# Graph network layer: scores and sums in four TensorE column groups of 16 nodes over three tiles, with norms by two chunks

## The chip, the cores and the metric

The kernel runs on one core of one Trainium2 chip. The metric is the device time of one execution in microseconds: the median of 3 runs for the kernel before. Profiles show one execution each; its engines are TensorE (PE, with PEld for its weight loads), VectorE (DVE), ScalarE (ACT), GpSimd (POOL) and SyncE (SP), whose queue issues most DMAs.

## What is computed

Two graph convolutions with attention (TransformerConv, two heads of 64) over 6250 nodes and 106250 edges, a batch norm with ReLU between them, then a residual and a layer norm. All is float32; the edges come sorted by their destination `dst`.

```python
def _transformer_conv(h, edge_attr, src, dst, Wq, bq, Wk, bk, Wv, bv, We, Ws, bs):
    q, k, v = ...                      # h @ W + b, (n, 2, 64) each
    e = (edge_attr @ We).reshape(-1, H, C)
    alpha = jnp.einsum('ehc,ehc->eh', q[dst], k[src] + e) / jnp.sqrt(C)
    ex = jnp.exp(alpha - segment_max(alpha, dst)[dst])
    a = ex / segment_sum(ex, dst)[dst]
    out = segment_sum((v[src] + e) * a[:, :, None], dst)
    return out.reshape(n, H * C) + h @ Ws + bs

edge_attr = concat([cos((last_update[src] - t)[:, None] * time_w + time_b), msg])   # 32 + 64 columns
h = relu(batch_norm(_transformer_conv(x, edge_attr, ..., conv 1)))
out = layernorm(x + _transformer_conv(h, edge_attr, ..., conv 2))
```

## The kernel before, in words

The 106250 edges are cut into NC = 104 chunks of CE = 1024, a chunk into T = 8 tiles of 128 edges. A chunk is answerable for NN = 64 nodes, that is 128 rows of (node, head). As edges are sorted, the nodes of a chunk lie close together, and a plan at the start (`tile_gnn_resnorm`, L1303) works out from `dst` the first node of each group of nodes (`nbs`). It also checks that each node's edges lie in the tiles that its group looks at. Where that doesn't hold, the program takes `general`, another way altogether; `ordered` (L660) is the way that the profile shows.

A chunk's 64 nodes stand in two groups of GN = 32, 64 rows each. Group 0 looks at the last tile of the chunk behind and tiles 0 to 3, group 1 at tiles 3 to 7 (`window`, L687): five tiles for each. The first and the last chunk have windows of their own.

`conv(c, ...)` (L710) runs twice, c = 0 and c = 1. Its loop is a pipeline written out by hand (L1025 on); in iteration k stand, in this order on each engine:

- `fetch` (L740) of chunk k + 4 (c = 0) or k + 3 (c = 1): SyncE reads the groups' first nodes into registers (`value_load`, L747) and issues the loads of edge attributes (L751), one of query tables for each group (`ftab`, L767), and in the second convolution the time encoding (`fz`, L770), the turned attributes (`fxT` from `et_d`, L772) and two of residual rows (`fr`, L775).
- `gather` (L777) of the same chunk: eight indirect DMAs, issued by GpSimd, one for each tile, that bring the rows of the source nodes (L782). They are spread over the iteration, each tied to a step of TensorE by a dependence, so that they keep its pace.
- `score` (L867) of chunk k, in two halves (u = 0 and 1) into one PSUM tile of two banks: each group's 64 rows against five tiles, first the gathered rows (`ft`, 128 deep), then the attributes (`et`, 112 deep). A group writes its own 64 columns of TensorE.
- `turn_weights` (L908) of chunk k - 1: five 128x128 transposes of the weights in two PSUM tiles, copied by ScalarE.
- `divide` and `finish_turn` (L934, L948) of chunk k - 2: sums over their denominators, then two transposes.
- `lowest` and `weigh` (L896, L903) of chunk k: a minimum over the scores on VectorE and an exponential on ScalarE, 640 columns each.
- `turn_in` (L843) of chunk k + 1, in two halves: transposes of the gathered rows, and in the first convolution of the attributes too, copied by ScalarE (L856, L862); the turned attributes are stored to `et_d` (L864) for the second convolution.
- `finish` (L957) of chunk k - 2: products with Wv and We. In the first convolution the node's skip values, third column of the table, are added, and two stores of 32 nodes each into `hT` are put on a list (`outgoing`). In the second the residual is added, the row centred and its square summed. The norms of ten chunks (LG = 10, `STARTS`) are finished together: one square root on ScalarE (L1005), a reciprocal, and then `store` (L1010) scales a chunk's rows and puts two stores of 32 rows on the list.
- `gather_sums` (L920) of chunk k - 1: weights times gathered rows and attributes, 225 columns, for two groups and five tiles.

`send()` (L729) takes the next store off the list and puts it into SyncE's queue. It is called at four fixed places of an iteration. Stores into `out` and into `hT` wait for the one before to have landed, since neighbouring groups may overlap.

`tables` (L621) makes the query tables block by block between these steps, `tab_d` in DRAM, three columns for each head of a node in the first convolution (against the gathered rows, against the attributes, and skip) and two in the second. After the last iteration of the second convolution comes a tail written out by hand (L1117 to L1151).

Of the kernel before, what the change touches and what calls it, by code (L numbers as in the profile page):

```python
# [7 lines left out]
F32 = mybir.dt.float32  # L8
# [39 lines left out]
GN = NN // 2  # L48
NC = 104
NG = 2 * NC  # L50
# [10 lines left out]
LG = 10  # L61
STARTS = (*range(0, 91, LG), 96, 100, 102, 103)
# [558 lines left out]
def tables(nc, pl, c, fT, b0, work, bank):  # L621

    o = work.tile([P, GE, H, 3 - c], F32, name="fo", tag="fo", bufs=1)
    for i, (a, b) in enumerate(pl.mats[c]):
        pg = bank()
        pl.step = nc.tensor.matmul(pg, a, fT, start=True, stop=True)  # L626
        if i == 2 * H:
            nc.scalar.activation(o[:, :, :, 2], pg[:, :, None].to_broadcast([P, GE, H]), AF.Identity, bias=b)
# [6 lines left out]
        if i == len(pl.mats[c]) - 1:  # L635
            nc.scalar.dma_start(pl.tab_d[c][:, b0 * GE:(b0 + 1) * GE], o)
# [23 lines left out]
def ordered(ctx: ExitStack, tc: tile.TileContext, pl, x, dst, edge_attr_64, conv2, bn_g, bn_b, out):  # L660
# [23 lines left out]
    def bounds(j):  # L684
        return max(0, N - GN * (NG - j)), min(N - NN, GN * j)

    def window(k, g):  # L687
        if k == 0:
            return range(3 * g, 3 * g + GT + 1)
        if k == NC - 1:  # L690
            return range(4 * g - 4, 4 * g + GT - 1)
        return range(GT * g - 1, GT * g + GT)
# [4 lines left out]
    nc.vector.memset(qpi, HALF_PI)  # L697

# [11 lines left out]
    def conv(c, extra, first_blocks=None):  # L710
# [8 lines left out]
        p_s = cs.enter_context(tc.tile_pool(name=f"fp_s{c}", bufs=1, space=bass.MemoryType.PSUM))  # L719
# [14 lines left out]
        groups = [slice(g * NN, (g + 1) * NN) for g in range(2)]  # L734
        halves = [slice(g * GN, (g + 1) * GN) for g in range(2)]
# [4 lines left out]
        def fetch(k):  # L740
            s = ch[k] = Plan()
            s.behind = ch.get(k - 1)
            s.nb = []
            for j in (2 * k, 2 * k + 1):
                lo, hi = bounds(j)
                s.nb.append(lo if lo == hi else N - GN * (NG - j) if j >= NG - 2 else
# [18 lines left out]
            s.tab = load.tile([P, NN * H, 3 - c], F32, name="ftab")  # L765
            for g, r in enumerate(groups):
                nc.sync.dma_start(s.tab[:, r], pl.tab_d[c][:, bass.ds(s.nb[g], GN)].rearrange("p n h w -> p (n h) w"))  # L767
            if c:
# [5 lines left out]
                for r, at in zip(halves, s.nb):  # L774
                    nc.sync.dma_start(s.r[r], res_d[bass.ds(at, GN), :])  # L775
# [91 lines left out]
        def score(k, u):  # L867

            s = ch[k]
            if u == 0:  # L870
                s.bank = p_s.tile([P, CE], F32, name="fps")
                s.ps = s.bank[:, CE - len(window(k, 0)) * P:]
                s.runs = [[], []]
                for g, r in enumerate(groups):
                    tiles = window(k, g)
# [633 lines left out]
```

## Time and profile before

| | us |
|---|---|
| median of 3 runs | 2253.65 (2251.95 to 2262.63) |
| the profiled execution, whole | 2255.35 |
| its span, first to last instruction | 2253.5 |
| mean granted TensorE clock | 0.934 of full |

```
## 2 busy tenths in 40 slices
PE   4888889978888988988878888888788887887865
POOL 3777777777777777777277777777777777777750
DMA  7776666656676667766397666666666666666641
```

The page gives each engine's busy time, its share of the span and its instructions; here the span in 40 slices, each digit a tenth. Issuing and waiting don't count as busy. The dip in slices 20 and 21 is the passage from the first convolution to the second. A row of a group of instructions has its line, engine and operation, what it writes and reads, its count, its busy time, the mean of one in ns, and then the idle time of the engine ahead of it with what ended it.

### The profile page before, as it was taken

The numbers are of one execution on the slowest core, as the hardware profiler recorded it, in microseconds if no ns is written. First come the engines' busy times: TensorE is split into PE (matmuls) and PEld (weight loads), VectorE is DVE, ScalarE is ACT, GpSimd is POOL, SyncE is SP. The second block draws the span as 40 slices with busy tenths as digits, with TensorE's granted clock in tenths as the row PEclk, the third lists the DMA queues.
The fourth block names the chain that finished last, engine by engine and source line by source line (L and its number), as shares of the span: only waits on it lengthen the run. The fifth ranks groups of instructions, "written<-read, shape, count | busy, mean of one in ns | idle before, by whom it ended". The sixth has DMA issues, their size and how long they took to land.

```text
span 2253.5 us, 44949 instructions
## 1 busy us (share of the span) xinstructions
PE 1852.5 (82%) x13283; PEld 1254.6 (56%) x13283; DVE 1148.7 (51%) x3686; ACT 1099.8 (49%) x1947; POOL 1590.8 (71%) x1683
## 2 busy tenths in 40 slices
PE   4888889978888988988878888888788887887865
PEld 3565666656665666666545565555554555554433
DVE  4766666766666667777454333333333333333322
ACT  1767676755655555666533434343333333333323
POOL 3777777777777777777277777777777777777750
PEclk9999999989999999999889999999999999999987
DMA  7776666656676667766397666666666666666641
GB/s 220 199 196 182 167 182 193 188 148 176 191 191 185 161 188 196 190 174 176 84 259 186 176 174 167 173 169 181 171 176 164 174 176 182 163 167 149 160 120 45
DMA packets 476600, 389.76 MB, mean 173 GB/s; under 512 B 295438, under 2 KB 422306, under 8 KB 473018
## 3 DMA queue, kind: packets, MB, share of 16 engines
q1 hardware_dynamic: 404262, 235.05, 38.7%
q0 software_dynamic: 53184, 109.45, 20.5%
q10 hardware_dynamic: 18900, 42.28, 5.2%
q8 instruction: 109, 1.79, 0.4%
q14 instruction: 145, 1.19, 0.2%
HBM read 271.26 MB, written 111.89 MB: 170 GB/s over the span
## 4 chain that ended last, share of the span: by engine, by line
DMA 23%; PE 21%; issue 4%; SPq 3%; DVE 3%; POOL 1%; ACT 1%; ACTq 0%; DVEq 0%; POOLq 0%
DMA fxT<-et_d 14%; PE fps L890 7%; DMA ff<-hn_d,fsrcs 5%; PE fpa L930 4%; PE fppt L916 3%; PE fpx L852 3%; DMA out<-fout 2%; SPq L767 1%; POOL ff L782 1%; PE fpo L986 1%; PE fpo L952 1%; PE fpg L626 1%; SPq L770 1%; DMA ff<-h_d,fsrcs 1%; DMA ff<-xv_d,fsrcs 1%
## 5 line engine op out<-in xcount | busy, mean ns | idle before, releaser
L782 POOL DMA_INDIRECT ff<-xv_d,fsrcs x831 | 798.9, 961 | 283.4 <-issue 91.4
L782 POOL DMA_INDIRECT ff<-hn_d,fsrcs x783 | 742.1, 948 | 267.1 <-issue 91.8
L930 PE MATMUL fpa<-ff,fpt 128*64 128x225 f32 x4176 | 461.7, 364 | 1.7 <-ACT fpt L917 1.7
L890 PE MATMUL fps<-fft,ftab 128*64 128x512 f32 (+1 forms) x1668 | 361.3, 462 | 49.9 <-DMA ftab<-tab_d 42.0
L856 ACT COPY fft<-fpx 128x512 f32<-128x512 f32 x404 | 235.5, 583 | 287.6 <-PE fpx L852 287.1
L930 PEld LDWEIGHTS fpa<-ff,fpt 128*64 128x64 f32 x4176 | 335.2, 140 | 59.4 <-issue 3.5
L955 DVE COPY fat<-fpo 128x256 f32<-128x256 f32 x208 | 88.4, 425 | 532.7 <-PE fpo L953 520.6
L917 ACT COPY fpt<-fppt 128x384 f32<-128x384 f32 (+1 forms) x416 | 156.7, 428 | 395.0 <-PE fppt L916 390.0
L852 PE MATMUL fpx<-fident,ff 128*128 128x128 f32 x1664 | 273.3, 295 | 53.1 <-DMA ff<-hn_d,fsrcs 44.7
L852 PEld LDWEIGHTS fpx<-fident,ff 128*128 128x128 f32 x1664 | 215.2, 152 | 68.9 <-DMA ff<-hn_d,fsrcs 53.9
L890 PE MATMUL fps<-fxT,ftab 112*64 112x512 f32 (+1 forms) x834 | 168.0, 476 | 97.1 <-DMA fxT<-et_d 97.1
L916 PEld LDWEIGHTS fppt<-fident,fs 128*128 128x128 f32 x1044 | 116.1, 146 | 178.6 <-issue 154.7
L890 PEld LDWEIGHTS fps<-fft,ftab 128*64 128x64 f32 x1668 | 132.4, 156 | 139.3 <-issue 96.7
L906 ACT ACTIVATE fs<-fps,fm 128x640 f32<-128x640 f32 x208 | 165.8, 797 | 39.6 <-DVE fm L901 37.7
L952 PE MATMUL fpo<-fident,fa 128*128 128x128 f32 x208 | 68.9, 331 | 139.3 <-DVE fa L940 137.2
L899 DVE TENSOR_REDUCE flow<-fps 128x1 f32<-128x640 f32 x208 | 170.1, 818 | 13.3 <-PE fps L890 13.3
L916 PE MATMUL fppt<-fident,fs 128*128 128x128 f32 x1044 | 168.6, 295 | 8.1 <-DVE fb L600 4.7
L890 PEld LDWEIGHTS fps<-fxT,ftab 112*64 112x64 f32 x834 | 59.7, 149 | 176.1 <-DMA fxT<-et_d 160.2
L890 PE MATMUL fps<-fet,ftab 112*64 112x512 f32 (+1 forms) x834 | 153.2, 434 | 0.0
L861 PE MATMUL fpe<-fident,ff 128*112 128x128 f32 x832 | 143.2, 301 | 2.4 <-DVE ff L839 2.2
L834 ACT ACT_TABLE_LOAD x82 | 105.2, 1283 | 76.0 <-issue 74.0
L827 DVE SCALAR_TENSOR_TENSOR farg<-fturns,farg 128x256 f32<-128x256 f32 x312 | 132.9, 426 | 10.7
(202 smaller groups left out, 2367.7 us busy)
## 6 DMA issues: line engine op xcount, KB each, us to landing
ff<-in_edge_attr SPq DMA_DIRECT2D x206, 256.0 KB
et_d<-fet SPq DMA_DIRECT2D x104, 448.0 KB
fxT<-et_d SPq DMA_DIRECT2D x104, 448.0 KB
tab_d<-fo ACTq DMA_DIRECT2D x13, 1536.0 KB
ftab<-tab_d SPq DMA_DIRECT2D x208, 96.0 KB
enc_d<-fzs SPq DMA_DIRECT2D x104, 128.0 KB
tab_d<-fo ACTq DMA_DIRECT2D x13, 1024.0 KB
ftab<-tab_d SPq DMA_DIRECT2D x208, 64.0 KB
```

The source lines that it names most:

```text
L782: row = nc.gpsimd.indirect_dma_start(out=f[:, t, (1 if c else 0):1 + D], out_offset=None, in_=(h_d[:N, :] if k < RAW else hn_d) if c else ...
L827: nc.vector.scalar_tensor_tensor(arg, turn, -part, arg, op0=OP.mult, op1=OP.add)
L834: nc.scalar.activation(z[:, :len(of)], arg[:, :len(of)], AF.Sin, bias=qpi)
L852: last = nc.tensor.transpose(px[:, t * P:(t + 1) * P], s.f[:, u * 4 + t, 1:1 + D], ident)
L856: nc.scalar.copy(s.ft[:, u * GE:(u + 1) * GE], px)
L861: last = nc.tensor.transpose(pe[:EC, t * P:(t + 1) * P], s.f[:, u * 4 + t, 1 + D:], ident)
L890: step = nc.tensor.matmul(s.bank[r, to:to + n], s.tab[:kd, r, i], (of.et if i else of.ft)[:kd, at:at + n], start=i == 0, stop=i == 1)
L899: nc.vector.tensor_reduce(low, s.ps, AX.X, OP.min)
L906: nc.scalar.activation(s.s[:, :s.ps.shape[1]], s.ps, AF.Exp, bias=s.bias, scale=-1.0)
L916: last = nc.tensor.transpose(pp[:, at:at + P], s.s[:, t * P:(t + 1) * P], ident)
L917: nc.scalar.copy(s.pt[:, t0 * P:t1 * P], pp[:, :(t1 - t0) * P])
L930: steps.append(nc.tensor.matmul(s.pa[r], s.pt[:, t * P + g * NN:t * P + (g + 1) * NN], f[:, i % T, 1:1 + D + EW], start=t == 0, stop=t == ...
```

## The change

Four groups of 16 nodes take the place of two of 32: 32 rows and 32 columns of TensorE each (GH), over three tiles: group g looks at tiles 2g - 1, 2g and 2g + 1. So scores, minimum, exponential and weights are 384 columns wide, not 640; a chunk's scores are made at one place, into one of two PSUM tiles of one bank, in an order that takes the groups in turn. The first nodes of two neighbouring groups lie at most 16 apart and can lie closer; then two groups hold the same nodes. A 0/1 matrix made for each chunk on VectorE (`sel`, from `target`, made once by `targets`) joins the groups' rows: `finish_turn` multiplies with it where it transposed before, and what comes out are 64 neighbouring nodes from the chunk's first. So residual rows are one load, `hT` and `out` one store a chunk. The skip column leaves the tables for a tensor of its own. Norms are finished by two chunks, with a small exponential (`spare`) right behind the square root, and the places of `send` and of the gathers' ties move. The plan works with four groups.

```diff
-GN = NN // 2
+NQ = 4
+GN = NN // NQ
+GH = P // NQ
+QE = CE // NQ
 NC = 104
-NG = 2 * NC
+NG = NQ * NC
...
-LG = 10
-STARTS = (*range(0, 91, LG), 96, 100, 102, 103)
+LG = 2
+STARTS = (*range(0, NC - 2, LG), NC - 2, NC - 1)
...
-    o = work.tile([P, GE, H, 3 - c], F32, name="fo", tag="fo", bufs=1)
+    o = work.tile([P, GE, H, 2], F32, name="fo", tag="fo", bufs=1)
     for i, (a, b) in enumerate(pl.mats[c]):
         pg = bank()
         pl.step = nc.tensor.matmul(pg, a, fT, start=True, stop=True)
         if i == 2 * H:
-            nc.scalar.activation(o[:, :, :, 2], pg[:, :, None].to_broadcast([P, GE, H]), AF.Identity, bias=b)
+            skip = work.tile([P, GE], F32, name="fskip", tag="fskip", bufs=1)
+            nc.scalar.activation(skip, pg, AF.Identity, bias=b)
+            nc.scalar.dma_start(pl.skip_d[:, b0 * GE:(b0 + 1) * GE], skip)
...
-        return max(0, N - GN * (NG - j)), min(N - NN, GN * j)
+        return max(0, N - GN * (NG - j)), min(N - GN if j % NQ else N - NN, GN * j)
 
     def window(k, g):
-        if k == 0:
-            return range(3 * g, 3 * g + GT + 1)
         if k == NC - 1:
-            return range(4 * g - 4, 4 * g + GT - 1)
-        return range(GT * g - 1, GT * g + GT)
+            return range(2 * g - 3, 2 * g + 1)
+        return range(max(2 * g - 1, 0 if k == 0 else -1), 2 * g + 2 + (k == g == 0))
...
+            none = gt.tile([P, NC], F32, name="fnone")
+            nc.vector.tensor_scalar(none, pg[:, 1, :NC], float(H), own, op0=OP.mult, op1=OP.is_le)
+            nc.vector.tensor_scalar(target, pg[:, 0, :NC], float(H), own, op0=OP.mult, op1=OP.add)
+            nc.vector.scalar_tensor_tensor(target, none, float(P), target, op0=OP.mult, op1=OP.add)
...
-        p_s = cs.enter_context(tc.tile_pool(name=f"fp_s{c}", bufs=1, space=bass.MemoryType.PSUM))
+        p_s = cs.enter_context(tc.tile_pool(name=f"fp_s{c}", bufs=2, space=bass.MemoryType.PSUM))
...
+            if c:
+                send()
             s.nb = []
-            for j in (2 * k, 2 * k + 1):
+            for j in range(NQ * k, NQ * k + NQ):
...
-            s.tab = load.tile([P, NN * H, 3 - c], F32, name="ftab")
+            s.tab = load.tile([P, NN * H, 2], F32, name="ftab")
             for g, r in enumerate(groups):
                 nc.sync.dma_start(s.tab[:, r], pl.tab_d[c][:, bass.ds(s.nb[g], GN)].rearrange("p n h w -> p (n h) w"))
+            if c == 0:
+                s.skip = load.tile([P, NN], F32, name="fsk")
+                nc.sync.dma_start(s.skip, pl.skip_d[:, bass.ds(s.nb[0], NN)])
             if c:
                 s.z = load.tile([P, T, TD], F32, name="fz", bufs=AHEAD)
                 nc.sync.dma_start(s.z, enc_d[k].rearrange("p (t d) -> p t d", d=TD))
                 s.et = ets[k % len(ets)]
                 nc.sync.dma_start(s.et, et_d[k])
                 s.r = load.tile([NN, D], F32, name="fr", bufs=6)
-                for r, at in zip(halves, s.nb):
-                    nc.sync.dma_start(s.r[r], res_d[bass.ds(at, GN), :])
+                nc.sync.dma_start(s.r, res_d[bass.ds(s.nb[0], NN), :])
+                send()
...
+            n = len(window(k, 0)) * P
+            s.ps = p_s.tile([P, GE], F32, name="fps")[:, :n]
+            todo = []
+            for g, r in enumerate(groups):
+                tiles, at = window(k, g), 0
+                for own in (False, True):
+                    part = [t for t in tiles if (t >= 0) == own]
+                    for i in range(2 if part else 0):
+                        todo.append((at, g, r, s if own else s.behind, i, tiles.index(part[0]) * P, part[0] % T * P, len(part) * P))
+                        at += len(part) * P
+            steps = []
+            for _, _, r, of, i, to, at, n in sorted(todo, key=lambda one: one[:2]):
+                kd = EC if i else D
+                steps.append(nc.tensor.matmul(s.ps[r, to:to + n], s.tab[:kd, r, i], (of.et if i else of.ft)[:kd, at:at + n],
+                                              start=i == 0, stop=i == 1))
+            half, step = steps[NQ - 1], steps[-1]
...
+            n = len(window(k, 0))
+            pp = p_tr.tile([P, GE], F32, name="fppt", tag="tr")
+            for t in range(n):
+                last = nc.tensor.transpose(pp[:, t * P:(t + 1) * P], s.s[:, t * P:(t + 1) * P], ident)
+            nc.scalar.copy(s.pt[:, :n * P], pp[:, :n * P])
...
-                    steps.append(nc.tensor.matmul(s.pa[r], s.pt[:, t * P + g * NN:t * P + (g + 1) * NN],
+                    steps.append(nc.tensor.matmul(s.pa[r], s.pt[:, t * P + g * GH:t * P + (g + 1) * GH],
                                                   f[:, i % T, 1:1 + D + EW], start=t == 0, stop=t == n - 1))
-            return steps[2], steps[5], steps[-1]
+            return steps[3], steps[7], steps[-1]
...
+            s.sel = small.tile([P, P], F32, name="fsel", bufs=2)
+            nc.vector.tensor_scalar(s.sel, place_of, target[:, k:k + 1], None, op0=OP.is_equal)
...
-            nc.tensor.transpose(s.po[:, 0], s.a[:, :D], ident)
-            nc.tensor.transpose(s.po[:, 1], s.a[:, EW:], ident)
+            nc.tensor.matmul(s.po[:, 0], s.a[:, :D], s.sel, start=True, stop=True)
+            step = nc.tensor.matmul(s.po[:, 1], s.a[:, EW:], s.sel, start=True, stop=True)
...
-                    nc.vector.tensor_add(res[r], heads[r, :, h], s.tab[r, ::H, 2])
+                    nc.vector.tensor_add(res[r], heads[r, :, h], s.skip[r])
...
-                    for r, at in zip(halves, s.nb):
-                        outgoing.append((hT[:, bass.ds(at, GN)], res[:, r]))
+                    outgoing.append((hT[:, bass.ds(s.nb[0], NN)], res))
...
+                if k < NC - 2:
+                    spare = small.tile([1, 1], F32, name="fspare", bufs=2)
+                    nc.scalar.activation(spare, pl.ones[0:1, 0:1], AF.Exp)
...
-            for r, to in zip(halves, at):
-                outgoing.append((out[bass.ds(to, GN), :], o[r]))
+            outgoing.append((out[bass.ds(at, NN), :], o))
...
-                send()
+                if not c:
+                    send()
+                elif not coming:
+                    send(2)
...
-                step = score(k, 0)[1] if on(k) else None
+                half, scored = score(k) if on(k) else (None, None)
                 if k >= -1 and not filling:
-                    bring((1,), step)
+                    bring((1,), half)
...
-                half, step = score(k, 1) if on(k) else (None, None)
-                if k >= -1 and not filling:
-                    bring((3,), half if c else step or half)
-                    if c:
-                        bring((4,), step)
-                send()
-                if on(k - 2):
-                    finish_turn(k - 2)
                 if on(k):
                     lowest(k)
+                if not c:
+                    send()
+                if on(k - 2):
+                    step = finish_turn(k - 2)
+                if k >= -1 and not filling:
+                    bring((3,), step)
                 step = turn_in(k + 1, 0) if on(k + 1) else None
-                if k >= -1 and not c or filling:
+                if k >= -1:
                     bring(range(5) if filling else (4,), step)
...
-                for _ in range(min(len(done), 4 if k >= NC else 2 if k > NC - 12 else 1)):
+                for _ in range(min(len(done), 2 if k > NC - 6 else 1)):
                     store(*done.pop(0))
-                if c:
-                    send()
...
-                spare = small.tile([1, 1], F32, name="fspare", bufs=1)
-                nc.scalar.activation(spare, pl.ones[0:1, 0:1], AF.Exp)
                 turn_in(last, 1)
-                score(last, 0)
-                score(last, 1)
+                score(last)
```

Left out are the plan's checks for four groups in `tile_gnn_resnorm` (eight picked columns of `dst` in place of four, rows of 416 in place of 208), the rest of `targets` (the distances of the first nodes, spread over 128 rows by eight products of one row) and changes of names.

168 lines of the change are left out of this document (85 added, 83 removed).

## Prediction

> **What bounds the kernel now.** I read the page first, for its spread of work over engines, and it points the wrong way.
>
> ```profile
> span 2253.5 us, 44949 instructions
> PE 1852.5 (82%) x13283; PEld 1254.6 (56%) x13283; DVE 1148.7 (51%) x3686; ACT 1099.8 (49%) x1947; POOL 1590.8 (71%) x1683
> ```
>
> TensorE looks like the bound and GpSimd (POOL) like the runner-up. So the second view is the one line that GpSimd works at, the row gathers of L782, then the same line by stage (us, busy us and count), then GpSimd in order of time.
>
> ```profile
> L782 POOL DMA_INDIRECT ff<-xv_d,fsrcs x831: 940/944/1188, 32.8 to 1084.7; - x167
> L782 POOL DMA_INDIRECT ff<-hn_d,fsrcs x783: 938/944/1707, 1183.5 to 2191.5; - x196
> L782 POOL DMA_INDIRECT ff<-h_d,fsrcs x48: 940/944/1986, 1121.7 to 1182.3; - x48
> ```
> ```profile
> 33.00:1086.00 1053.00, 798.68 (x831) 0.94 0.67 181
> 1121.00:1250.00 129.00, 97.86 (x100) 0.90 0.82 218
> 1250.00:1460.00 210.00, 159.05 (x168) 0.93 0.65 170
> 1700.00:2140.00 440.00, 319.84 (x339) 0.96 0.64 167
> 2140.00:2193.00 53.00, 31.21 (x34) 0.87 0.47 118
> ```
> ```profile
> 1121.67 0.94 POOL L782 DMA_INDIRECT ff<-h_d,fsrcs  x1 [36.07 <-issue]
> 1122.92 0.94 POOL L782 DMA_INDIRECT ff<-h_d,fsrcs  x1 [0.30 <-issue]
> ...
> 2185.19 0.94 POOL L782 DMA_INDIRECT ff<-hn_d,fsrcs  x1 [2.54 <-PE fps L890]
> ```
>
> A gather is 0.94 us, and 0.30 us lie ahead of it even where nothing is waited for: from start to start 1.25 us. There are 831 + 783 + 48 = 1662, eight to a chunk of 1024 edges, and 1662 x 1.25 = 2077 us of a span of 2253.5. The stages say how near each is to that pace: 1053/831 = 1.27 us in all of the first convolution, 210/168 = 1.25 early in the second, but 440/339 = 1.30 from 1700 on and 53/34 = 1.56 at its end. So GpSimd's pace of 10.0 us a chunk binds; 71% hides it, since the 0.30 count as idle. What is left over is 32.8 us ahead of the first gather, 36.1 between the convolutions, 2253.5 - 2192.4 = 61.1 after the last (2191.5 and its own 0.9), and the loss late in the second convolution: 1070.7 us from 1121.7 to 2192.4, where 831 x 1.25 = 1038.7 would do.
>
> That loss has one origin, in SyncE's queue (SP), which works its entries in order:
>
> ```profile
> 1985.61 4.91 SPq L732 DMA_DIRECT2D out<-fout  x2
> 1992.05 0.41 SPq L751 DMA_DIRECT2D ff<-in_edge_attr  x1
> 1992.66 0.96 SPq L767 DMA_DIRECT2D ftab<-tab_d  x2
> ...
> 1994.15 0.42 SPq L772 DMA_DIRECT2D fxT<-et_d  x1
> 1994.76 0.85 SPq L775 DMA_DIRECT2D fr<-res_d  x2
> 1995.79 4.47 SPq L732 DMA_DIRECT2D out<-fout  x2
> ```
> ```profile
> SPq L732 <- DMA out<-fout: 372.8, 117, 5.9
> ...
> PEld fps L890 <- DMA fxT<-et_d: 160.2, 70, 3.5
> ```
>
> Two stores of a chunk stand side by side; the second waits until the first has landed (372.8 us in 117 waits). From store to store the queue takes 1995.79 - 1985.61 = 10.18 us and has no rest in it: it is full, it falls behind, the loads come as they are needed (the scores wait 160.2 us for fxT), and gathers that keep step with the scores wait too (2.54 us at 2185.19).
>
> **The change part by part.**
>
> *Steady pace of GpSimd.* The gathers stay as they are: same number, same size, tied to other steps of TensorE. That term, 2077 us, the change can't touch. All that it saves on TensorE is hidden under it while the pace holds.
>
> *TensorE.* First whether column groups run side by side:
>
> ```profile
> 38.74 1.13 PE L626 MATMUL fpx<-fxT,fm 128*128 128x512 f32 x2 [0.17 <-ACT fo L630]
> ...
> 1989.35 1.08 PE L890 MATMUL fps<-fxT,ftab 112*64 112x512 f32 x4 [1.07 <-DMA fxT<-et_d]
> ```
> ```profile
> L930 PE MATMUL fpa<-ff,fpt 128*64 128x225 f32 x4176 | 461.7, 364 | 1.7 <-ACT fpt L917 1.7
> ```
>
> One product of 512 columns over the whole array (two records) takes 1.13 us; two such products in the two halves take 1.08. So groups of 64 columns run at once. Four of 32 the trace doesn't show; between one and four at once, I take four, nearest to that pair. Scores: 2 x 640 columns a group become 2 x 384, so 2.1 us of streaming (1.08 less a tail of some 0.2 for 512 columns) becomes 1.3. Sums: 461.7/208 = 2.2 us a chunk for 10 records a group becomes 1.3 for 6. Five transposes of weights become three (some 0.2 less), and the two transposes after the division become two-record products (some 0.2 more). About 1.7 us less a chunk, worth nothing in the steady stretch. If only two ran at once, scores and sums would be 2.6 and 2.25 us, 0.5 more than now, still under the gathers.
>
> *VectorE.* One more comparison of 128x128 a chunk, beside a shorter minimum over 384 columns.
>
> ```profile
> L824 DVE TENSOR_SCALAR fturns<-farg 128x256 f32<-128x256 f32 x104 | 36.1, 347 | 3.5
> L782 POOL DMA_INDIRECT ff<-xv_d,fsrcs x831 | 798.9, 961 | 283.4 <-issue 91.4 <-PE fpx L852 34.5 <-DMA fwv<-in_L_gnn_Wv 29.5
> L782 POOL DMA_INDIRECT ff<-hn_d,fsrcs x783 | 742.1, 948 | 267.1 <-issue 91.8 <-PE fps L890 54.8 <-PE fpx L852 31.8
> ```
>
> By half of L824's 347 ns it costs some 0.2 us. The gathers of the first convolution, which has some nine more such operations a chunk, are 13 ns longer; eight times 13 ns, by a ninth, is 0.01 us a chunk. I add 1 us to each convolution (0 to 8).
>
> *SyncE.* A chunk's fetch gets two more value loads and two more table loads.
>
> ```profile
> L747 SPq TENSOR_LOAD <-nbs x410: 260/268/1353, 29.9 to 2202.1; - x137
> ```
>
> With the address arithmetic beside each (an estimate: 0.3 us by a value load, 0.04 by a table load of 0.96/2), that is 2 x 0.57 + 2 x 0.52 = 2.2 us. One load of fr and one store go (1.0 us less), and so does the wait, since consecutive stores are now a whole chunk apart. Without its wait of some 4 us the queue now needs 6.1 us; after, 7.3 of 10.0. In the first convolution a load of the skip rows comes too and one store of hT goes. It gains nothing there, and the queue has room. With that the queue is on time and the second convolution falls back to the pace: 1038.7 + 4 for its first stage (129 - 100 x 1.25) + 1 = 1043.7 in place of 1070.7, **-27** (-30 to -8).
>
> *DMA.* Table rows of 768 and 512 B become 256 B, twice as many.
>
> ```profile
> q1 hardware_dynamic: 404262, 235.05, 38.7%
> ```
>
> A packet of q1 takes 0.387 x 16 x 2253.5/404262 = 34.5 ns; 256 more a chunk are at most 0.55 us of 10 on 16 engines that are 64 to 67% busy. Below, it is nothing, as the bytes fall. No cost.
>
> *Norms by two chunks.* 52 square roots in place of 13, each with two table switches on ScalarE.
>
> ```profile
> 1986.02 1.28 ACT L1005 ACT_TABLE_LOAD   x1
> 1987.31 0.21 ACT L1005 ACTIVATE fvar<-fvar 64x10 f32<-64x10 f32 x1
> ...
> 1700.00:2140.00 440.00, 356.82 (x2576) 222.46 (x2574) 146.65 (x540) 157.00 (x364) 319.84 (x339) 0.96 0.64 167
> ```
>
> 2 x 1.28 + 2 x 0.21 = 3.0 us every second chunk. ScalarE is 157.0 of 440 us busy there, 3.6 us a chunk; a chunk with a switch then has 6.6 of 10. Hidden under the gathers; behind it in ScalarE's queue wait the copies of fpt and fft, for which TensorE waits. ScalarE: Activation LUTs, "What ACT_TABLE_LOAD costs", in the Trainium skill, gives 2.66 us a switch, a drain being half of it. The trace disagrees: the next activation starts 1.29 us after the load did.
>
> *Ahead of the first gather.* The plan takes 8 more such records and longer rows on VectorE:
>
> ```profile
> 13.78 1.55 PE L1404 MATMUL ppick<-fident,picked 104*1 104x104 f32 x8 [1.74 <-DVE picked L1400]
> ```
>
> **+2** us (0 to 4). The matrices' targets are made after it, under the gathers' head start of four chunks.
>
> *Between the convolutions*, from the chain of waits:
>
> ```profile
> 1085.97 0.85 PE fpx L852 x4
> ...
> 1095.30 0.44 PE fpx L852 x4
> ...
> 1110.66 1.73 DMA fhT<-fres
> 1112.41 1.71 DMA fhT<-fres
> ```
>
> No gathers cover TensorE here. One of the two stores of hT goes (-1.7), and the last chunk's scores (7 tiles to 4), sums and transposes shorten by some 3: **-5** (-9 to 0).
>
> *After the last gather.* Now the loads of the last chunks are late; on time, the last gather lands after 2.5 us, is turned, and waits for ScalarE's norms (3.0) and two scalings: 10 us to the last fft copy. From there it is 2253.5 - 2226.4 = 27.1 us now:
>
> ```profile
> 2226.44 0.56 ACT L856 COPY fft<-fpx 128x512 f32<-128x512 f32 x1
> ...
> 2227.05 5.95 PE fps L890 x16
> ...
> 2238.87 3.10 PE fpa L930 x28
> ```
>
> Scores at 512/896 columns (-2.5), sums at 8 of 14 records a group (-1.3), minimum, exponential and transposes at 4/7 (-1.3): 22. So 32 in place of 61.1, **-29** (-32 to -10).
>
> *Sum*: +2 +1 -27 -5 -29 = -58; span 2253.5 - 58 = 2195.5. The profiled run took 2255.35, 1.85 more than its span, and 1.7 more than the median of 2253.65; with both, **2196 us**, or -2.6%.
>
> **The rivals.**
>
> 1. *Half of it* (16%): loads are on time later, or the end stays longer; -13 and -15 in place of -27 and -29, some 2224. For it speaks that both gains hang on one queue.
> 2. *SyncE stays full* (6%): the change doesn't free it. A value load takes up to 1.35 us; were all four at that, the queue needs 7.3 + 4.3 = 11.6. Then only -3 is left: 2251. Against it: the median is 0.27.
> 3. *ScalarE's switches take the gathers' place* (5%, slower): 39 more pairs, 3.0 us each, fully exposed are 117 us on the 2196: 2313. It decides once a chunk's chain, from the last gather's landing through fft, scores, exponential and fpt to the sums, has less than 3.0 us to spare in 10. Against it: at 1986 such a load stood in ScalarE's queue and the gathers kept step. By the skill's 2.66 the same exposure would be 39 x 2 x 2.66 = 207 us, an estimate.
> 4. *TensorE's clock falls* (4%): with less to do it waits longer; after a wait four transposes took 0.85 us, not 0.44 (rows above). If that held all through the second convolution, some 5.6 busy us a chunk would become 10.5 and 0.5 x 104 = 52 us come back: 2248. TensorE: Matmul & The Clock Gate, Part 1, in the Trainium skill, has this rule (half clock after an idle window). Against it: once busy again, at 1095.30, it was back at 0.44.
> 5. *Groups of 32 run one at a time* (3%): 3072 and 2700 columns in turn are 5.2 and 4.5 us, with the rest over 12 a chunk: some 2700.
>
> **How the numbers follow.** My forecast has 66%, between 2183 (all good ends: -9 -30 -32, none added) and 2215. With rival 1 that is 82%; the range of 2182 to 2236 leaves some 20% out. Chances, with 0.5% (11 us, about what can be told from no change): faster 66 + 16 + 1 = 0.83, same 0.09 (2, 4 and the worst of 1), slower 0.08 (3 and 5).
>
> **What would show it.** Right: 1662 gathers, again 1.25 us apart from 1250 to the end; the last one starts at some 2160; some 32 us after it; the wait of stores for stores falls from 372.8 to under 40; scores wait little for fxT; scores 1.5 and sums 1.3 us a chunk with four records starting together; 52 loads for the square root. Wrong: gathers waiting for TensorE at over 1.27 a piece; a gap on TensorE ended by ScalarE's fpt or fft in every second chunk; DMA share over 0.8; a first gather after 38.

## The result and the profile after

The changed kernel takes **2232.88 us** (median of 4 runs, 2229.36 to 2236.11), the kernel before 2254.11 beside it (4 runs); the ratio is 0.9899, with a 95% interval of 0.9868 to 0.9929. The forecast was 2196 us; of the 58 us foretold 21 came. (On three later occasions, those of e1 to e4 and e13 to e16, the kernel before itself took 2655 to 2682 us, so the whole times of these runs stand only beside each other.) The profiled run of the changed kernel took 2234.6 us, with a span of 2232.8 and a mean granted TensorE clock of 0.851, where it was 0.934.

The page's head first, in the columns of the one before:

```profile
span 2232.8 us, 50017 instructions
...
PE 1624.1 (73%) x14961; PEld 1142.1 (51%) x14961; DVE 1154.7 (52%) x3998; ACT 1109.0 (50%) x1906; POOL 1592.5 (71%) x1684
```

TensorE lost 228 us of busy time, which is more than the whole gain; GpSimd's work is the same. So the gathers come next: their line by table gathered from (count, shortest, median and longest in ns, first and last start), then by stage (us, busy us, count, granted clock, DMA share, GB/s).

```profile
L817 POOL DMA_INDIRECT ff<-xv_d,fsrcs x831: 940/944/1194, 61.2 to 1113.8; - x167
L817 POOL DMA_INDIRECT ff<-hn_d,fsrcs x783: 938/944/1406, 1215.5 to 2197.1; - x196
L817 POOL DMA_INDIRECT ff<-h_d,fsrcs x48: 938/944/1842, 1150.1 to 1211.1; - x48
```
```profile
1150.00:1250.00 100.00, 73.31 (x75) 0.79 0.73 203
1250.00:1460.00 210.00, 157.32 (x167) 0.87 0.70 186
1700.00:2140.00 440.00, 332.70 (x353) 0.83 0.67 174
2140.00:2199.00 59.00, 44.07 (x47) 0.83 0.57 142
```

From 1700 on there are 353 gathers in 440 us, 1.25 us each, where there were 339; and it stays so to the last one (47 in 59 us). The late loss is gone. But the first gather starts at 61.2 us, not at 32.8. The lines of GpSimd in order of time show what stands there (the bracket holds the idle time ahead of an entry and what ended it), and lines of waits (us in total, times, longest) tell who held whom:

```profile
47.05 0.24 POOL L703 IOTA fplace<- 128x128 f32 x1 [43.79 <-DMA skip_d<-fskip]
61.23 1.11 POOL L817 DMA_INDIRECT ff<-xv_d,fsrcs  x1 [13.94 <-DVE fbits L793]
62.64 0.94 POOL L817 DMA_INDIRECT ff<-xv_d,fsrcs  x1 [0.31 <-issue]
...
2197.15 0.95 POOL L817 DMA_INDIRECT ff<-hn_d,fsrcs  x1 [0.30 <-issue]
```
```profile
POOL fplace L703 <- DMA skip_d<-fskip: 43.8, 1, 43.8
```
```profile
SPq L783 <- DVE ftarget L728: 25.7, 1, 25.7
...
SPq L763 <- DMA out<-fout: 10.0, 6, 3.2
```
```profile
PE fpo L980 <- DVE fsel L968: 321.9, 135, 11.0
...
PE fps L918 <- DMA fxT<-et_d: 2.4, 1, 2.4
```

and in the kernel before:

```profile
PE fps L890 <- DMA fxT<-et_d: 97.1, 68, 2.5
```

Two new things stand ahead of the gathers, and neither is a long piece of work. The iota that makes the row of column numbers takes 0.24 us, but GpSimd is idle for 43.8 us ahead of it, till a store of the plan has landed at 47.05. (In the kernel before it was idle for 29.5 us and then went straight to the first gather.) And SyncE's first load of edge rows, like the first gather, which writes the same tile ff, waits for VectorE, which has finished the targets at 60.4 us. The lines on stores and on fxT are the good news: the stores' wait for stores has fallen from 372.8 to 10.0 us, and that of the scores' matmuls for fxT from 97.1 to 2.4 (the forecast shows that of their weight loads, PEld, 160.2).

The line on fsel is new, and it is the largest sum among the waits of TensorE's matmuls: 321.9 us for the comparison that makes `sel`. The comparison stands directly behind the division on VectorE, for which TensorE waited 137.2 us in the kernel before, so this is the wait for the division and some 0.3 us more each time. It costs the gathers nothing that shows: 241.0 us of it lie in the first convolution, which takes as long as before (1052.6 us between first and last gather, for 1051.9).

SyncE's queue now has rests in it, as its entries late in the second convolution show:

```profile
1992.56 0.40 SPq L783 DMA_DIRECT2D ff<-in_edge_attr  x1
1993.18 1.98 SPq L799 DMA_DIRECT2D ftab<-tab_d  x4
...
1996.33 0.50 SPq L809 DMA_DIRECT2D fr<-res_d  x1
2000.01 0.54 SPq L763 DMA_DIRECT2D out<-fout  x1
2003.22 0.41 SPq L783 DMA_DIRECT2D ff<-in_edge_attr  x1
```

Between 1996.8 and 2000.0 the queue issues nothing. TensorE's groups, last (busy us, mean ns of one, then the idle time ahead of them), with the new table loads:

```profile
L956 PE MATMUL fpa<-ff,fpt 128*32 128x225 f32 x5008 | 328.3, 402 | 0.1
L918 PE MATMUL fps<-fft,ftab 128*32 128x384 f32 (+2 forms) x2080 | 237.3, 448 | 4.6 <-ACT fft L891 4.0 <-DMA ftab<-tab_d 0.6
...
L1033 ACT ACT_TABLE_LOAD x52 | 66.7, 1283 | 0.9
```
```profile
2199.26 1.35 PE L956 MATMUL fpa<-ff,fpt 128*32 128x225 f32 x24
```

Four groups of 32 columns do run side by side: 24 records of 0.4 us end within 1.35 us. Over the whole run the sums take 328.3/208 = 1.58 us a chunk, for 1.3 foretold and 2.2 before; the lower clock has its part in that (e5 below has 332.2 us for them at a clock of 0.859, e8 314.6 at 0.916).

### The profile page after: what moved, and what is told of

It is laid out like the page before. It is cut to its first block, busy times and chain, and to the rows that moved or that the text cites. A ratio compares the mean times of both kernels' runs of the same rounds, so it can differ in the third digit from the quotient of the medians.

```text
span 2232.8 us, 50017 instructions
## 1 busy us (share of the span) xinstructions
PE 1624.1 (73%) x14961; PEld 1142.1 (51%) x14961; DVE 1154.7 (52%) x3998; ACT 1109.0 (50%) x1906; POOL 1592.5 (71%) x1684
## 4 chain that ended last, share of the span: by engine, by line
PE 23%; DMA 19%; DVE 5%; issue 4%; POOL 2%; ACT 1%; SPq 1%; DVEq 0%; POOLq 0%; ACTq 0%
DMA ff<-hn_d,fsrcs 17%; PE fpa L956 6%; PE fps L918 4%; PE fpx L887 4%; PE fpg L629 3%; POOL ff L817 2%; PE fpo L1014 2%; PE fpo L1015 1%; PE fpo L980 1%; DMA ff<-xv_d,fsrcs 1%; PE fppt L942 1%; PE fpo L981 1%; PE fpg L1286 1%; DVE fa L966 1%; DVE ff L973 1%
## 5 line engine op out<-in xcount | busy, mean ns | idle before, releaser
L980 PE MATMUL fpo<-fsel,fa 128*128 128x128 f32 x416 | 104.5, 338 | 322.7 <-DVE fsel L968 321.9
L956 PE MATMUL fpa<-ff,fpt 128*32 128x225 f32 x5008 | 328.3, 402 | 0.1
L918 PE MATMUL fps<-fft,ftab 128*32 128x384 f32 (+2 forms) x2080 | 237.3, 448 | 4.6 <-ACT fft L891 4.0
L956 PEld LDWEIGHTS fpa<-ff,fpt 128*32 128x32 f32 x5008 | 155.2, 121 | 96.9 <-issue 35.9
L896 PEld LDWEIGHTS fpe<-fident,ff 128*112 128x112 f32 x832 | 133.6, 172 | 18.4 <-DVE ff L874 8.8
L918 PE MATMUL fps<-fxT,ftab 112*32 112x384 f32 (+2 forms) x1040 | 133.9, 440 | 2.4 <-DMA fxT<-et_d 2.4
L918 PEld LDWEIGHTS fps<-fft,ftab 128*32 128x32 f32 x2080 | 108.9, 118 | 48.4 <-issue 12.5
L897 ACT COPY fet<-fpe 112x512 f32<-112x512 f32 x208 | 123.7, 595 | 16.5 <-PE fpe L896 15.2
L918 PE MATMUL fps<-fet,ftab 112*32 112x384 f32 (+2 forms) x1040 | 130.9, 423 | 0.0
L926 DVE TENSOR_REDUCE flow<-fps 128x1 f32<-128x384 f32 x208 | 115.2, 554 | 24.2 <-PE fps L918 22.6
```

Of the source, the lines that this page charges most:

```text
L896: last = nc.tensor.transpose(pe[:EC, t * P:(t + 1) * P], s.f[:, u * 4 + t, 1 + D:], ident)
L897: nc.scalar.copy(s.et[:, u * GE:(u + 1) * GE], pe[:EC])
L918: steps.append(nc.tensor.matmul(s.ps[r, to:to + n], s.tab[:kd, r, i], (of.et if i else of.ft)[:kd, at:at + n], start=i == 0, stop=i == 1))
L926: nc.vector.tensor_reduce(low, s.ps, AX.X, OP.min)
L956: steps.append(nc.tensor.matmul(s.pa[r], s.pt[:, t * P + g * GH:t * P + (g + 1) * GH], f[:, i % T, 1:1 + D + EW], start=t == 0, stop=t == ...
L980: nc.tensor.matmul(s.po[:, 0], s.a[:, :D], s.sel, start=True, stop=True)
```

## The experiments

"Early" below is the changed kernel with both holds at the start mended. In the diffs "-" is the kernel that the experiment starts from.

**The start: e1 to e3, e5, and e13 to e16.** The iota moves among the plan's constants (A), the temporaries of the targets get buffers of their own (B), and early is both:

```
A -    place_of = const.tile(...); nc.gpsimd.iota(place_of, ...)          # top of ordered
  +    got.place_of = keep.tile(...); nc.gpsimd.iota(got.place_of, ...)   # in the plan, behind lane_i
B -    lane, away, none = gt.tile(...)       # pool "fgt", closed when targets() ends
  +    lane, away, none = const.tile(...)
```

*A alone* (e1; again as e13 and e16):

> The row of column numbers (fplace) is made with the plan's other constants, so GpSimd has nothing ahead of the gathers; the temporaries of the matrices' targets stay where they were. Theory (two holds one behind the other: the iota waited till 47.1 us for the plan's buffers, and after it the gathers wait for the targets, whose buffers the edge rows take over, till 60.4): the second hold alone is enough, first gather still at 60 to 62 us, total 2229 to 2237. Rival (the iota alone is to blame): first gather at some 34 us, total some 2205.

> The iota among the plan's constants, the targets' temporaries where they were; the first try fell on an occasion on which the kernel before took 2682 us, where its first gather started at 60.9. Theory (the targets' buffers alone hold the gathers till some 61 us, whatever the iota does): total as the changed kernel, 0.987 to 0.994 of the kernel before, 2226 to 2237. Rival (the iota's hold is what costs): 2204 to 2212.

> Third try of the kernel with the iota among the plan's constants and the targets' temporaries where they were; first gather at 60.9 and 61.0 in the two tries so far. Theory (the targets' buffers alone hold the gathers): total as the changed kernel, 2226 to 2240. Rival: 2204 to 2212.

```profile
60.94 1.11 POOL L816 DMA_INDIRECT ff<-xv_d,fsrcs  x1 [57.50 <-DVE fbits L792]
```

First gather at 60.9, 61.0 and 62.0: as with the iota in its place. The targets alone hold it.

*B alone* (e2; again as e14 and e15):

> The temporaries of the targets get buffers of their own; the iota stays behind the branch. Theory (two holds): the iota holds the gathers till some 47 us, first gather at 47 to 49, total 13 us below the changed kernel's 2233, some 2219 to 2221. Rival (the targets' buffers alone are to blame): 34 us and 2205. Rival (the pace of the rest is set elsewhere and takes the earlier start back): 2230 or more.

> Buffers of their own for the targets' temporaries, the iota behind the branch; in the first try the first gather started at 48.3. Theory (the iota alone holds the gathers till 48, so 16 of the 28.5 us): 16 us above the kernel with both mended (2206), 2217 to 2226. Rival (a later start is made up on the way): 2204 to 2210.

> Third try of the kernel with buffers of their own for the targets' temporaries and the iota behind the branch; in the two tries so far the kernel before itself took 2682 and 2655 us, and the first gather started at 48.3 and 48.4. Theory (the start comes through to the end microsecond for microsecond): 16 us above the kernel with both mended (2206), 2217 to 2226, or 0.984 to 0.990 of the kernel before. Rival (a later start is made up on the way): 2204 to 2210.

```profile
47.41 0.24 POOL L703 IOTA fplace<- 128x128 f32 x1 [44.14 <-DMA skip_d<-fskip]
48.28 1.11 POOL L817 DMA_INDIRECT ff<-xv_d,fsrcs  x1 [0.64 <-issue]
```

First gather at 48.3, 48.4 and 47.8: the iota alone holds it till 47.4. So the holds run beside each other, and the later end counts: mending the targets leaves 48.3 - 32.8 = 15.5 of the 28.5 us, mending the iota leaves all. The six runs took 2678 to 2717 us, beside 2655 to 2682 for the kernel before, so what was expected of their whole time (2217 to 2240 us) stays open, and with it how far a start at 48 comes through to the end where the kernel before takes 2250.

*Both* (e3, then e5 again):

> Both: the iota among the plan's constants, and buffers of their own for the targets' temporaries. Theory: first gather at 33 to 37 us as in the kernel before, the rest as in the changed kernel, so 2233 - 26 = 2203 to 2210. Rival (TensorE at its lower clock, or the loads, set the pace and take the earlier start back): 2225 to 2233 in spite of a first gather at 34.

> The same kernel as in the run before of this name (iota among the plan's constants, buffers of their own for the targets' temporaries), on an occasion on which the kernel before takes its usual 2254 us and not 2682. Theory: first gather at 33 to 37 us, the gathers 1.25 us apart to the end, total 2203 to 2210 (0.977 to 0.981 of the kernel before). Rival (something else takes the earlier start back): 2225 to 2233.

```profile
32.17 1.11 POOL L816 DMA_INDIRECT ff<-xv_d,fsrcs  x1 [28.72 <-DMA fwv<-in_L_gnn_Wv]
```

First gather at 32.6 in e3, 32.2 in e5, which took **2206.49 us** (0.9836 of the kernel before, 0.9785 to 0.9888). That is 26 us below the changed kernel for a start 29 us earlier. Beside its own kernel before (2245.04) it is 38.6 us less, where the changed kernel was 21.2 less, a step of 17 us, and the two intervals overlap; so the whole times leave 17 to 26. The traces say more. From the first to the last gather's start e5 takes 2166.8 - 32.2 = 2134.6 us and the changed kernel 2197.1 - 61.2 = 2135.9, and behind the last start 34.7 and 35.7: here nothing on the way takes the early start back. On the occasion of e1 to e3 most of it was taken back: 2715.79, 2704.65 and 2702.47 us, 13 us for a start 28 us earlier (e1 to e3) and 2 for one 16 us earlier (e2 to e3), and e3 was 1.0074 of the kernel before. Why isn't known.

**The norms: e7.** Early, with the norms by ten chunks again:

```
- LG = 2;  STARTS = (*range(0, NC - 2, LG), NC - 2, NC - 1)
+ LG = 10; STARTS = (*range(0, 91, LG), 96, 100, 102, 103)      # and two scalings a chunk from 92 on, not 98
```

> The changed kernel with the early start (iota among the plan's constants, buffers of their own for the targets' temporaries), and the norms by ten chunks again, so 39 pairs of table switches fewer, 117 us of ScalarE's time. Theory (the switches stand beside the gathers and cost nothing before the last one): gathers 1.25 us apart as before, total 2200 to 2212, as with norms by two (2206), the difference only in the tail. Rival (each switch delays fft and fpt and so the gathers): 20 us or more faster, under 2190.

```profile
L1032 ACT ACT_TABLE_LOAD x13 | 16.7, 1283 | 0.2
```

2206.90 us (0.9797, 0.9768 to 0.9825), with 13 loads for the square root in place of 52: the same time as early, as far as can be told (the two ratios' intervals overlap). The 39 extra pairs of switches show no cost, and norms by two no gain.

**TensorE: e8.** Early, with every score matmul issued twice:

```
-  for _, _, r, of, i, to, at, n in sorted(todo, ...):
+  for _, _, r, of, i, to, at, n in 2 * sorted(todo, ...):
```

> The same early start, and every score matmul issued twice into the same columns, the second with the result of the first overwritten: 1.5 us more of TensorE in each of 208 chunks, 312 us in all. Theory (TensorE has over 2 us to spare in a chunk of 10): total 2206 to 2225, what is added lying in the tail and between the convolutions, gathers at 1.25 us. Rival (TensorE is the bound, and the change's columns count one for one): 2400 to 2518.

```profile
L917 PE MATMUL fps<-fft,ftab 128*32 128x384 f32 (+2 forms) x4160 | 465.7, 434 | 5.1 <-ACT fft L890 4.0 <-DMA ftab<-tab_d 0.6 <-ACT fft L888 0.3
```
```profile
1700.00:2140.00 440.00, 359.86 (x3897) 242.24 (x3897) 158.36 (x635) 198.47 (x405) 332.70 (x353) 0.90 0.65 173
```

2208.67 us (0.9812, 0.9784 to 0.9839): 2 us above e5 and e7, so twice the scores cost nothing that can be told from noise. TensorE is busy 359.86 of 440 us (first column after the stretch) and the gathers keep 353 in 440. So what the change saves on TensorE is hidden, as the forecast had it. The mean granted clock rose from 0.859 to 0.916 with the added work.

**SyncE's queue: e4 and e6, then e10 and e9.** Does the late loss come of the two out stores side by side, or of TensorE's columns? First the kernel before, with one store ahead of a chunk's loads and one behind them:

```
  def fetch(k):
+     if c: send(2 if k > NC - 12 else 1)         # first store
      ... value loads, ff, ftab, fz, fxT; if c: fr ...
+     if c: send(2 if k > NC - 12 else 1)         # second store
      # the other send() calls of convolution 2 go, but for a send(4) once all chunks are fetched
```

> The kernel before with its two groups of 32 nodes and its norms by ten chunks; in convolution 2 the two out stores of a chunk stand apart on SyncE, one ahead of a chunk's loads and one behind them, and not side by side. Theory (the late loss of the kernel before comes of the second store's wait for the first in SyncE's queue, not of TensorE's columns): the waits of a store for a store fall from 322 us between 1150 and 2150 to under 60, the gathers keep 1.25 us to the end (last one at some 2165 to 2175), and the total is 2203 to 2218. Rival (TensorE's work did it): 2245 to 2255.

> The kernel before, with groups of 32 nodes and norms by ten chunks; only the two out stores of a chunk stand apart on SyncE, one ahead of a chunk's loads and one behind them. The first try fell on an occasion on which the kernel before itself took 2682 us. Theory (the late loss of the kernel before is SyncE's second store waiting for the first, not TensorE's columns): waits of a store for a store fall from 372.8 us to under 60, the gathers keep 1.25 us to the end (last one at 2165 to 2175, not 2191), and the total is 2203 to 2225, depending on how long its longer tail is. Rival (TensorE's fewer columns brought it): 2245 to 2255.

```profile
1600.53 0.41 SPq L753 DMA_DIRECT2D ff<-in_edge_attr  x1
...
1604.75 5.62 SPq L732 DMA_DIRECT2D out<-fout  x2
1611.90 0.42 SPq L753 DMA_DIRECT2D ff<-in_edge_attr  x1
```

2248.04 us (0.9986, 0.9970 to 1.0002): no gain, and the stores wait 364.5 us for each other, as before. Here the theory seemed to fall; but SyncE's entries above show that the edit hadn't done what it was for. Nothing else is issued between the last entry of one fetch and the first of the next, so the second store of a chunk and the first of the next one met, still "x2" in one line. So e6 decides nothing. (e4 is the same kernel: 2681 us beside 2682, again no difference.) In e10 the first store stands behind the edge rows' load:

```
+     ... value loads, ff;  if c: send(2 if k > NC - 12 else 1)
+     ... ftab, fz, fxT, fr;  send(2 if k > NC - 12 else 1)
```

> The kernel before with its two out stores of a chunk truly apart: one between the edge row load and the table loads, one behind the last load, so that other issues lie on both sides (in the earlier try the last one of a chunk and the first of the next met again). In the last 12 chunks two go at each place. Theory (SyncE's wait of store for store makes the late loads): those waits fall from 322 to under 150 us between 1150 and 2150, the gathers from chunk 56 of convolution 2 on lose under 8 us up to the last four chunks instead of 18, and the total falls by 10 to 25 us (0.989 to 0.996), the tail staying as long. Rival (they are late for another reason): no change, 0.997 to 1.003.

```profile
1611.57 0.40 SPq L751 DMA_DIRECT2D ff<-in_edge_attr  x1
1614.08 0.33 SPq L732 DMA_DIRECT2D out<-fout  x1
...
1616.66 0.85 SPq L777 DMA_DIRECT2D fr<-res_d  x2
1617.75 0.34 SPq L732 DMA_DIRECT2D out<-fout  x1
```
```profile
SPq L732 <- DMA out<-fout: 129.2, 91, 3.8
```
```profile
L785 POOL DMA_INDIRECT ff<-hn_d,fsrcs x783: 940/944/1705, 1186.3 to 2165.9; - x196
```

**2208.48 us** (0.9826, 0.9796 to 0.9856), with TensorE's work, groups and norms of the kernel before: the wait falls from 372.8 to 129.2 us, the last gather starts at 2165.9 in place of 2191.5, and even the end, which was expected to stay, shrinks to 2203.7 - 2165.9 = 37.8 us from 62.0. It is 41.5 us below the kernel before beside it (2249.99), past the 10 to 25 expected: stores sent from other places bring twice what the whole change did. And the other way round, early with its 64 rows in two stores side by side:

```
-  outgoing.append((out[bass.ds(at, NN), :], o))
+  for r in (slice(0, NN // 2), slice(NN // 2, NN)):
+      outgoing.append((out[bass.ds(at, NN), :][r], o[r]))     # both sent behind the loads
```

> The changed kernel with the early start, but its 64 out rows of a chunk go in two stores of 32 rows side by side behind the chunk's loads, as in the kernel before; TensorE's work is the changed one. Theory (the second store waits for the first to land, 3.7 us a chunk on SyncE, and this makes the last third's loads late): the waits of a store for a store are over 250 us again, the gathers fall behind 1.25 us in the last third, the tail grows, total 2225 to 2255. Rival (the late loss of the kernel before was TensorE's): 2204 to 2212 in spite of such waits.

```profile
1702.74 4.62 SPq L762 DMA_DIRECT2D out<-fout  x2
1710.04 0.41 SPq L780 DMA_DIRECT2D ff<-in_edge_attr  x1
1710.65 3.15 SPq L796 DMA_DIRECT2D ftab<-tab_d  x4
...
1715.70 3.40 SPq L762 DMA_DIRECT2D out<-fout  x2
1722.15 0.42 SPq L780 DMA_DIRECT2D ff<-in_edge_attr  x1
```
```profile
SPq L762 <- DMA out<-fout: 301.8, 107, 4.4
```
```profile
PE fps L915 <- DMA fxT<-et_d: 124.9, 68, 3.6
```
```profile
1700.00:2140.00 440.00, 287.64 (x304) 0.81 0.58 154
```

2356.65 us (1.0488, 1.0456 to 1.0520), 150 us above early and past both theories' numbers: from one edge rows' load to the next SyncE now takes 12.1 us, where the gathers need 10, and they fall to 440/304 = 1.45 us. The stores wait for stores again (301.8 us), and the scores' matmuls for fxT (124.9 us, 97.1 in the kernel before). The direction is the theory's; its size was too small. The stores' waits are no longer than in the kernel before (372.8 us), whose queue took 10.18 us a chunk, so the rest must come from the queue's other entries; that these are the four value loads and four table loads a chunk, for two and two, is argued, not tried. With its stores side by side the change would have been a loss.

**What lies under the gathers: e11 and e12.** Half of the indirect gathers, in the kernel before and in early:

```
+ near = hn_d if c else pl.xv_d            # fetch, chunks 8 to 102: one plain load for the odd tiles
+ nc.sync.dma_start(f[:, 1:T:2, ...], near[:4 * P, :].rearrange("(t p) d -> p t d", p=P))
+ if 8 <= k < NC - 1 and t % 2: continue   # gather
```

> The kernel before with half of the indirect gathers: from chunk 8 on the odd tiles of a chunk take the first 512 rows in one plain load from SyncE instead of the rows that the edges name, so the numbers that come out are others; every other instruction is left. GpSimd then needs 5 of the 10 us a chunk. Theory (only the gathers hide TensorE): the kernel falls to what TensorE's chain allows, some 9 us a chunk, 1900 to 2080. Rival (loads or SyncE are as near to the bound as the gathers): 2150 or more.

> The same cut of the gathers (odd tiles from chunk 8 on take the first 512 rows in one plain load, so other numbers come out) in the changed kernel with the early start. Theory (the change's saving on TensorE is real and lies under the gathers): TensorE's busy time a chunk is 7.4 us against 8.2, so 1780 to 1950, and 5 to 12% under the kernel before with the same cut. Rival (the narrow groups save nothing on TensorE, its lower clock or SyncE's longer queue eats it): within 2% of the kernel before with the same cut.

The kernel before, then early:

```profile
L787 POOL DMA_INDIRECT ff<-xv_d,fsrcs x451: 938/944/1162, 32.8 to 924.8; - x151
L787 POOL DMA_INDIRECT ff<-hn_d,fsrcs x403: 938/943/1712, 1034.3 to 2027.9; - x135
L787 POOL DMA_INDIRECT ff<-h_d,fsrcs x48: 940/944/1863, 973.0 to 1033.0; - x48
```
```profile
L821 POOL DMA_INDIRECT ff<-xv_d,fsrcs x451: 938/945/1245, 33.4 to 1025.7; - x151
L821 POOL DMA_INDIRECT ff<-hn_d,fsrcs x403: 938/944/1872, 1137.2 to 2005.3; - x135
L821 POOL DMA_INDIRECT ff<-h_d,fsrcs x48: 940/945/1898, 1069.7 to 1131.0; - x48
```
```profile
PE fpo L984 <- DVE fsel L972: 210.8, 94, 6.2
```

2090.50 and 2051.00 us (0.9300 and 0.9124 of the full kernel before; 1.9% apart). e11's time lies between its theory's 2080 and its rival's 2150. e12's theory (1780 to 1950 us, 5 to 12% below e11) falls; its rival (within 2%) stands. The sum hides two differences of opposite sign. In the second convolution the kernel before gains hardly anything, 2027.9 - 973.0 = 1055 us, with 337.6 us of stores waiting for stores: SyncE, at 10.1 us from one chunk's first load to the next (1604.70 to 1614.85, without a rest), was as near a bound as the gathers. Early takes 936 there. But in the first convolution early is *slower*, 992 us for 892. In the kernel before, TensorE hardly rests there: it is busy for 680.65 of the 700 us from 200 to 900; in early it is busy for 619.95 of the 800 from 200 to 1000. It waits 210.8 us in that convolution (line above) for the comparison behind the division, where the kernel before waits 24.6 us for the division. What makes VectorE late there, the comparison, its place behind other work, or the changed order of the steps, wasn't tried. Under whole gathers the same wait is there, as shown above, and hidden.

## Why the prediction came out as it did

The terms, from start to start of gathers, forecast and measured:

| term | forecast | measured | how |
|---|---|---|---|
| ahead of the first gather | +2 | +28.5 | 61.23 - 32.77 |
| first convolution | +1 | +0.7 | (1113.8 - 61.2) - (1084.7 - 32.8) |
| between the convolutions | -5 | -0.7 | 35.35 for 36.07 idle |
| second convolution | -27 | -22.8 | (2197.1 - 1150.1) - (2191.5 - 1121.7) |
| after the last start | -29 | -26.4 | (2232.8 - 2197.15) - (2253.5 - 2191.5) |
| sum | -58 | -20.7 | 2232.8 - 2253.5 |

*The step that failed* is "Ahead of the first gather": "**+2** us (0 to 4). The matrices' targets are made after it, under the gathers' head start of four chunks." The term measured +28.5. The step counted the plan's added work by its length, took the targets for work beside the gathers, and didn't name the iota. Both are short, 0.24 us for the iota and under 5 us for the targets on VectorE; what they cost is the wait that they put ahead of the gathers, once through GpSimd's order (the iota stands before the first gather) and once through memory (the edge rows' buffers take over the bytes of the targets' temporaries, so SyncE's load and the gather wait for the targets, and these come behind the features' transposes). e1, e2 and e5 show each hold alone and neither. Both were to be read from the code: one is an instruction's place on an in-order engine, the other a pool that closes just before the next one opens. And the trace of the kernel before shows the first hold, on an engine where it cost the gathers nothing. `qpi`, a constant in the pool that the iota's tile joins, is VectorE's first work behind the branch, and it waits there for the plan's last store:

```profile
48.41 0.06 DVE L697 MEMSET qpi<- 128x1 f32 x1 [4.86 <-DMA tab_d<-fo]
```

The text's own sign, "a first gather after 38", is what told it.

*Right*: the gathers' pace binds, and TensorE's saving is hidden under it (e8: twice the scores, the same time). That saving was 228.4/208 = 1.1 us of busy time a chunk, not the 1.7 foretold, which the time doesn't show. The +1 of the first convolution came in at +0.7, but by luck: it priced the comparison at its own length, and TensorE's long wait there is hidden only because the gathers bind. The late loss and most of the long end came from SyncE's queue, and one store a chunk frees it. That was an argument; e10 and e9 show it, e10 by giving the same gain without any of the change's TensorE work. The term of -27 came in at -22.8, since the late stage went back to its pace in full but the first one of that convolution lost 100 - 75 x 1.25 = 6.2 us, some 2 more than the 4 allowed for, and the next one a gather or so. The Trainium skill's DMA: Bandwidth & Descriptors, "Anatomy of one DMA", puts a fixed 2 us on a transfer (on GpSimd's path), most of it the receipt of the last write, longest where the write goes to HBM. The trace agrees in kind, with a larger number, on SyncE's queue: a 16 KB store kept its neighbour waiting for 372.8/117 = 3.2 us. That a smaller store would hardly be sooner done, as a fixed part has it, no run here shows.

*Too hopeful*: between the convolutions, -0.7 for -5. The bound given went to 0. In the chain of waits the second store of hT is gone as foretold (1.7 us), and a chunk's sums are down from 2.05 to 1.3 us, but the passage is as long as it was. What takes their place stays open: no run changes this passage alone.

*The rivals.* Of "half of it" (2224) the time is the nearest, but not for its reason: the loads were on time. "SyncE stays full" did not come, and e9 shows that it would have with a second store side by side. "ScalarE's switches" show no cost (e7). "TensorE's clock falls" did come (0.934 to 0.851, and 0.83 in the late stage) and left the gathers' pace as it was (353 in 440 us). TensorE: Matmul & The Clock Gate, Part 1, in the Trainium skill, says that activity releases the throttle; e8 agrees in direction, with 0.916 for more work against 0.859. "One at a time" fell: 24 records in 1.35 us.

With the start mended, e5's 2206.5 lies 10 us above the 2196 forecast. e5, e7 and e10 take 1.6 to 2.0% less than the kernel before beside them, the changed kernel 1.0% less (e5's interval still reaches into that kernel's); e10 does it by the places of its stores alone.

## What to carry to other kernels

An instruction that is added costs its wait, not its length: before calling one hidden, read what stands behind it on its engine, and whose memory its buffers take or leave, above all at a seam where one pool closes and the next opens. When an in-order DMA queue is full, look first for an entry that waits inside it (here a store for a store): moving it past other entries freed as much as the rewritten computation did with its start mended. And look in the trace that an experiment did what it was meant to, before its time is believed; e6 would have thrown out a theory that was right.

## What the runs showed of the hardware that was not expected

- Less work lowered TensorE's granted clock, 0.934 to 0.851, and doubled scores raised it to 0.916, with the same pace of gathers (353 in 440 us). So a busy share (73% in place of 82%) compares work done at different clocks: the same sums took 332.2 us at 0.859 and 314.6 at 0.916.
- A wait of 321.9 us of TensorE for VectorE cost nothing under whole gathers. With half of the gathers, where that wait was 210.8 us in the first convolution (up to 6.2 us each), the kernel with less TensorE work was the slower one there (992 for 892 us).
